# Two adapters of neighbouring half batches in one Gelu task, with a plan of newer durations and newly drawn ranks

## The chip, the cores and the metric

One core of a Trainium2 chip runs the whole kernel in float32. The time is device microseconds of one execution, and of several runs the median counts. The core has five engines with queues of their own: TensorE (PE, matmuls), VectorE (DVE), ScalarE (ACT, which evaluates functions from tables), GpSimd (POOL) and SyncE (SP), which here issues the transfers (DMA). Each engine runs its queue strictly in the order in which the program was written, and waits where a result or a buffer is not there yet.

## What is computed

Eight sequences of 512 tokens with 256 channels pass through four layers. Cut to what matters:

```python
# layer 0, a transformer block with a modulated norm; 16 heads of 16 channels
x = ln(src) * (1 + scale(timestep)) + shift(timestep)
scores = q @ k.T / 4 + attention_bias            # bias: (8, 16, 512, 512)
scores = where(src_mask, -inf, scores)
x = x + softmax(scores) @ v @ Wo + bo
h = ln(x) * g2 + beta2
x = x + gelu2(h @ W1 + b1) @ W2 + b2             # 256 -> 1024 -> 256, gelu2(z) = z*sigmoid(1.702 z)
# layers 1 and 3, the two adapters, each with its own weights
hidden = gelu(x @ down_W.T + down_b)             # 256 -> 64, exact Gelu
hidden = expert_W[idx] @ hidden + expert_b[idx] + domain_emb[idx]   # one of 16 experts a sequence
x = ln(hidden @ up_W.T + up_b + x) * ln_gamma + ln_beta
# layer 2, between the adapters: pairs of channels are rotated by theta and phi of the sequence
```

The first adapter's norm weights and the rotation of layer 2 are folded into one pair of rows for each sequence (`rot`), so a first adapter ends with the rotated tokens and a second one with the output.

## The kernel before

The work is cut by sequence `b`, by half (256 query tokens, two tiles of 128), by group `g` of four heads, and by tile: 8 x 2 x 4 x 2 = 128 units, numbered `n`. `attention` (L908) does one unit: four bias tiles are fetched (L918), the mask is added on POOL (L922), scores are made on PE (L930), subtracted and reduced on DVE (L942), exponentiated on ACT (L946). The result is turned, for two of four heads by PE transposes (L981, all four heads in the first sequence's first three groups) and for the others by DVE and a transfer (L957, L966); every second unit the values are multiplied in (L1007). `prepare` (L778) makes the norm, queries, keys and values of the next sequence.

After every eighth unit, `finish` (L1174) takes the two tiles of a half through the output projection, the feed-forward (L1041, its activations by Tanh at L1070), the first adapter and the second adapter (`adapter`, L1097), and stores them (L1196). The last half is finished one tile at a time (L1299). An adapter with number `l` does, in order:

- at the first half of a sequence, one matmul that joins the chosen expert with the up projection (`eu`, L1103),
- a transpose of the tokens (L744, copied at L702), the down projection (L1116),
- a Gelu for each of the two tiles (L1124), one task of the plan with the mode "gelu",
- the up projection (L768), added to the tokens on DVE (L1133), then statistics (L710 to L719) and norm (L732),
- for `l` = 0 the rotation (L1152, L1156, L1167 or on POOL), for `l` = 1 the norm's weights (L1143).

Nothing is written in the order in which it runs. Every piece is a task with an engine (or a choice of two), a duration, what it reads and writes, and a rank; `Plan.run` (L156) simulates the engines once at build time, gives an engine that comes free the ready task of the lowest rank whose buffers can be had, and the tasks are emitted in that order. Ranks follow the unit: an attention unit's are around `n`; those of a `finish` are spread over n + 2 to n + 11, or n + 19 from n = 100 on, in proportion to its PE work (`Plan.end`, L128, called after L1294). `Plan.stir` (L147) then shifts the ranks in given stretches by random amounts from given seeds; a list of 21 such draws stands at L1303. The plan's constants for transfers are `AFTER[DMA]` (time until a landed transfer is seen), `BACKLOG`, and 1.5 us of landing (L170, L226). The plan counts 1.41 us whenever ACT changes between the modes "exp" and "gelu".

Buffers that matter here come from rings: `HID` has 2 (Gelu outputs), `EU` 2, `HT` 2 (transposed tokens), `RES` 4 (a sequence's tokens), `ROT` 1, and eight PSUM banks, four for scores and four for the rest, which may borrow from the former.

Of the kernel before, what the change touches and what calls it, by code (L numbers as in the profile page):

```python
# [20 lines left out]
P = 128  # L21
# [4 lines left out]
NF = FF // P  # L26
# [4 lines left out]
TURNED = 2  # L31
# [49 lines left out]
class Plan:  # L81

    AFTER = {PE: 0.22, DVE: 0.14, ACT: 0.16, POOL: 0.12, DMA: 2.2}
    BACKLOG = 9.0
    FLIGHT = 8

# [67 lines left out]
    def run(self, free_at):  # L156
        ready = {e: [] for e in free_at}
        mode = dict.fromkeys(free_at)
        events, order, seq = [], [], 0
        for n, t in enumerate(self.tasks):  # L160
            t.n = n
            if t.waits == 0:
                heapq.heappush(events, (t.at, seq, "ready", t))
                seq += 1
        for e, at in free_at.items():
            heapq.heappush(events, (at, seq, "free", e))
            seq += 1
        idle = set()
        now, queues = 0.0, self.BACKLOG
        landed = [self.BACKLOG + 1.5] * self.FLIGHT  # L170
        while events:
            now, _, what, x = heapq.heappop(events)
            if what == "ready":
                for e in x.costs:

                    later = 1.0 if e == DVE and ACT in x.costs else 0.0
                    heapq.heappush(ready[e], (x.rank + later, x.n, x))
            elif what == "free":
                idle.add(x)
            elif what == "over":  # L180
                for b in x.buffers:
                    b.left -= 1
                    if b.left == 0:
                        b.home.free.append(b.slot)
            if events and events[0][0] == now:
                continue
            for e in [e for e in free_at if e in idle]:
                held, short = [], set()
                while ready[e]:
                    entry = heapq.heappop(ready[e])  # L190
                    t = entry[2]
                    if t.engine is not None:
                        continue
                    new = [b for b in t.buffers if b.slot is None]
# [12 lines left out]
                    held.append(entry)  # L207
                else:
                    t = None
                for h in held:  # L210
                    heapq.heappush(ready[e], h)
                if t is None:
                    continue
                for b in new:
                    b.home, b.slot = b.slots.take()
                t.engine, cost = e, t.costs[e]
                if t.mode is not None and t.mode != mode[e]:
                    cost += 1.41 if e == ACT else 0.1
                    mode[e] = t.mode
                idle.discard(e)  # L220
                if e == DMA:
                    begun = now
                    for _ in range(t.many):
                        begun = max(begun, landed[-self.FLIGHT]) + cost / t.many
                        queues = max(queues, begun) + t.data / t.many
                        landed.append(queues + 1.5)  # L226
# [22 lines left out]
def conditioned_sequence_kernel(  # L249
# [320 lines left out]
    def late_weights():  # L570
        wo_rows = w_o.rearrange("(c u j e) n -> c j u e n", c=NC, u=2, e=32)

        def load(rank, cost, data, emit, key, many=1):
# [7 lines left out]
        load(3.0, 3.6, 1.0, lambda: [  # L581
            nc.sync.dma_start(wo[32 * j : 32 * j + 32, c], wo_rows[c, j, :, :HD])
            for c in range(NC) for j in range(4)
        ], "wo", many=8)
# [10 lines left out]
    def rotations():  # L595
# [63 lines left out]
            nc.sync.dma_start(wu[A1:K1, 1], turned_rows)  # L659

        plan.rank = 6.8
        plan(DMA, 1.6, bias_rows, ["turned_rows"], ["wu"], data=0.6, many=4)
        plan.rank = 7.0
        ps = Buffer(BG, lambda t: t[:, : NC * (B + 1)].rearrange("p (c b) -> p c b", c=NC))

# [242 lines left out]
    def attention(u, n):  # L908
# [7 lines left out]
        dif = [Buffer(BIAS) for _ in range(4)]  # L916
        for j in range(4):
            plan(DMA, 0.54, lambda j=j: nc.sync.dma_start(  # L918
                dif[j].t, bias[b, 4 * g + j, qt * P : (qt + 1) * P, :]), [], [dif[j]], data=0.8)
# [49 lines left out]

        if turned:  # L970
            plan(DMA, 2.75, moved, [(tb, j) for j in range(turned)], [(pT, i)],
                 data=1.05 * TURNED, many=4)
        plan.rank = n + 0.0

        whole = "p (j k i q c) -> p j k i q c"
# [119 lines left out]
    eus, rots = {}, {}  # L1095

    def adapter(b, l, res, rk, ts):  # L1097
        n, w = len(ts), len(ts) * P
        rows = slice(ts[0], ts[0] + n)
        if ts[0] == 0:  # L1100

            ps, eu = Buffer(BG, lambda t: t[:A1, :D]), Buffer(EU)
# [1 line left out]
                ps.t, ewT[l][: A1 + 1 + 7 * l, b, :], wu[: A1 + 1 + 7 * l, l, :], start=True,  # L1104
                stop=True), [("ewT", l), "wu", *rk], [ps], mode="full")
            evict(lambda ps=ps: (eu.t, ps.t), [ps], [eu], 0.35, 0.35)
            eus[l] = eu
        eu = eus[l]
        xT, xk = half_transposed(lambda t: res.t[:, t, :], rk, ts)
        ps, hid = Buffer(BG, lambda t: t[:, :P]), Buffer(HID)  # L1110


        def down():
            for c in range(NC):
                for i in range(n):
# [2 lines left out]
                        start=(c == 0), stop=(c == NC - 1),  # L1118
                    )

        def hidden():
            for i in range(n):
                lanes = slice(A * i, A * i + A)
# [2 lines left out]
                    bias=db[lanes, b : b + 1] if l else db[lanes, B:],  # L1126
                )

        plan(PE, 0.52, down, [*xk, "wd"], [ps], mode="down")
        plan(ACT, 0.27 * n, hidden, [ps, "hid1", "db"], [hid], mode="gelu")  # L1130

        def add(ps):
            nc.vector.tensor_tensor(res.t[:, rows], ps, res.t[:, rows], ALU.add)  # L1133
# [7 lines left out]
        if l == 1:  # L1141
            for r, op in enumerate((ALU.mult, ALU.add)):
                plan(DVE, 0.06 + 0.27 * n, lambda r=r, op=op: nc.vector.tensor_tensor(  # L1143
                    hat.t if r == 0 else res.t[:, rows], hat.t, rows_of(rows2, r, n), op),
                    hk if r else ["rows2"], rk if r else hk)
            return


# [25 lines left out]
    def finish(b, ts, store=None):  # L1174
# [13 lines left out]
        if ts[0] == 0:  # L1188
# [14 lines left out]
    def experts_matrices():  # L1203
# [19 lines left out]
        for b in range(B):  # L1223
# [10 lines left out]
                            "o p a -> (o p) a"),  # L1234
                    )

            plan(DMA, 2.0, fetch, ["expert"], [(raw, b)], data=0.2, many=2)

        def kept():
            nc.gpsimd.tensor_tensor(  # L1240
# [43 lines left out]
    for n, u in enumerate(units):  # L1284
# [5 lines left out]
        if n % 8 == 7:  # L1290
            half = n // 8 % 2
            if n + 1 < len(units):
                plan.begin()
                finish(u[0], [2 * half, 2 * half + 1])  # L1294
                plan.end(n + 2.0, n + (11.0 if n < 100 else 19.0))
                continue

            for t in range(2):
                plan.begin()  # L1299
                finish(u[0], [2 + t], Buffer(PT, lambda p: p.rearrange(  # L1300
                    "p (c q) -> p c q", q=2 * P)[:, :NF]) if t else None)
                plan.end(n + 2.0 + 4 * t, n + 11.0 + 4 * t)
    plan.stir([  # L1303
        (410212, 1.8, 6.8, 0.15),
        (199711, 113.2, 123.2, 0.5),
        (682069, 101.9, 121.9, 0.3),
        (105905, 1.0, 6.0, 0.15),
        (778456, 99.8, 104.8, 0.3),
        (979319, 99.1, 139.1, 0.5),
        (907673, 48.8, 68.8, 0.5),  # L1310
        (22724, 102.9, 107.9, 0.5),
        (298360, 122.0, 132.0, 0.3),
        (628414, 41.2, 51.2, 0.5),
        (243383, 126.2, 166.2, 1.0),
        (212106, 116.9, 136.9, 0.3),
        (595484, 120.3, 140.3, 0.15),
        (163641, 56.0, 66.0, 0.3),
        (54223, 41.6, 46.6, 0.15),
        (562752, 129.4, 169.4, 0.5),
        (467595, 24.0, 29.0, 0.3),  # L1320
        (266067, 61.1, 66.1, 0.3),
        (728061, 32.7, 42.7, 0.15),
        (41169, 28.2, 38.2, 0.3),
        (751015, 16.0, 26.0, 0.3),
    ])
    order = plan.run({PE: 1.5, DVE: 2.6, ACT: 3.6, POOL: 1.6, DMA: 5.0})
    for task in order:
# [95 lines left out]
```

## Time and profile before

| | us |
|---|---|
| three runs | 891.4, 893.95, 889.95 (median 891.4) |
| the profiled execution, of which the span | 890.14, 888.4 |
| mean granted TensorE clock | 0.989 of full speed |
| Exp (L946) 512 x 721 ns | 343.6 on ACT |
| copies of transposes (L702) 226 x 584 ns | 125.5 on ACT |
| Gelu (L1124) 64 x 362 ns | 23.2 on ACT |
| mask add (L922) 512 x 1161 ns | 580.3 on POOL |
| ACT waiting for DVE's minimum before an Exp | 45.6, 43 times |
| DVE waiting for scores (L942 for L930) | 31.4, 32 times |
| PE's weight loads waiting for an Exp (L981 for L946) | 20.3, 30 times |
| ACT waiting for a down projection (L1124 for L1116) | 3.4, 5 times |
| transfers, busy share of 16 engines | 78% |

Busy shares are averages over the span. A "wait" is idle time of an engine in front of an instruction, with what ended it; it costs something only where that instruction is on the path to the end, and the chain of work that ended last shows one such path. The 40 slices of the page show a full middle, a dip of the granted clock in the third and fourth slices, and an end in which DVE, ACT and POOL thin out:

```profile
PE   9998999999999999999999999999999999999994
PEld 7654675666666666656666666666666566666683
DVE  4757799989999999988998999899999999999766
ACT  5974779979898998979988897988979789799653
POOL 8867999999899898999889997998899999999432
PEclk9998999999999999999999999999999999999997
DMA  9577887698986988888896978968897898998400
```

### The profile page before, as it was taken

Reading aid. Unit: us, or ns where it says so; the run is one execution under the profiler, and the core shown is the slowest. Engines: PE = TensorE matmul, PEld = TensorE weight load, DVE = VectorE, ACT = ScalarE, POOL = GpSimd, SP = SyncE. Lnnn points to the kernel's source line nnn. Section 1 sums busy time; section 2 is a strip of 40 time slices with the busy share of each in tenths; the row PEclk is TensorE's granted clock in tenths of the full one; section 3 lists DMA queues with packets and bytes.
Section 4 is the critical chain, followed back from the end, with each engine's and each line's share of the span. In section 5 each row is a group of like instructions: output and inputs, shape, how many; then the busy total and the mean of one; then the engine's idle time right before and its main releaser. Section 6 shows DMA issues by size and latency. Waiting matters only on the chain.

```text
span 888.4 us, 20406 instructions
## 1 busy us (share of the span) xinstructions
PE 860.4 (97%) x6430; PEld 565.8 (64%) x6430; DVE 783.0 (88%) x2141; ACT 740.7 (83%) x1349; POOL 775.3 (87%) x907
## 2 busy tenths in 40 slices
PE   9998999999999999999999999999999999999994
PEld 7654675666666666656666666666666566666683
DVE  4757799989999999988998999899999999999766
ACT  5974779979898998979988897988979789799653
POOL 8867999999899898999889997998899999999432
PEclk9998999999999999999999999999999999999997
DMA  9577887698986988888896978968897898998400
GB/s 319 156 226 229 281 254 227 205 293 246 288 276 203 314 276 271 295 243 247 250 317 206 282 238 266 318 202 287 242 309 236 267 284 260 297 298 276 107 25 24
DMA packets 163214, 218.54 MB, mean 246 GB/s; under 512 B 19167, under 2 KB 93961, under 8 KB 163106
## 3 DMA queue, kind: packets, MB, share of 16 engines
q1 hardware_dynamic: 163062, 217.22, 78.0%
q8 instruction: 51, 0.84, 0.4%
q14 instruction: 57, 0.47, 0.2%
q10 hardware_dynamic: 44, 0.02, 0.0%
HBM read 149.89 MB, written 4.24 MB: 173 GB/s over the span
## 4 chain that ended last, share of the span: by engine, by line
PE 56%; ACT 14%; DVE 10%; DMA 8%; POOL 7%; issue 3%; SPq 2%; POOLq 0%; DVEq 0%; ACTq 0%
PE bank L1086 10%; PE bank L930 9%; PE bank L981 8%; PE bank L1061 7%; PE bank L1007 7%; POOL bias L922 5%; DMA bias<-in_bias 5%; ACT bias L946 5%; PE bank L820 4%; DVE bias L942 3%; PE bank L768 3%; ACT pT L702 2%; PE bank L744 2%; PE bank L858 2%; PE bank L419 1%
## 5 line engine op out<-in xcount | busy, mean ns | idle before, releaser
L922 POOL TENSOR_TENSOR bias<-bias,neg 128x512 f32<-128x512 f32 x512 | 580.3, 1161 | 42.3 <-DMA bias<-in_bias 28.2
L946 ACT ACTIVATE bias<-bias,low 128x512 f32<-128x512 f32 x512 | 343.6, 721 | 46.2 <-DVE low L942 45.6
L942 DVE CUSTOM_DVE_ANT_0 bias<-bank,bias 128x512 f32<-128x512 f32 x512 | 328.4, 679 | 42.7 <-PE bank L930 31.4
L981 PEld LDWEIGHTS bank<-shifted,bias 128*128 128x128 f32 x1120 | 124.9, 141 | 77.8 <-ACT bias L946 20.3
L981 PE MATMUL bank<-shifted,bias 128*128 128x128 f32 x1120 | 158.2, 279 | 7.8 <-ACT bias L946 3.2
L957 DVE STREAM_TRANSPOSE tb<-bias 128x512 f32<-128x512 f32 x232 | 155.6, 693 | 4.5 <-ACT bias L946 3.9
L702 ACT COPY pT<-bank 128x512 f32<-128x512 f32 x226 | 125.5, 584 | 35.9 <-PE bank L981 34.1
L930 PE MATMUL bank<-kT,qz 32*128 32x512 f32 x1024 | 149.4, 645 | 0.0
L1007 PE MATMUL bank<-pT,v_pad 128*32 128x256 f32 x1120 | 126.0, 386 | 0.9 <-ACT bias L946 0.9
L1061 PE MATMUL bank<-hT,w 128*128 128x256 f32 (+1 forms) x544 | 125.1, 373 | 1.1 <-ACT hT L754 0.6
L1086 PE MATMUL bank<-w,gT 128*128 128x256 f32 x496 | 119.5, 384 | 0.0
L1007 PE MATMUL bank<-pT,v_turn 128*32 128x256 f32 x928 | 113.1, 386 | 2.0 <-DMA pT<-tb 0.8
L1061 PEld LDWEIGHTS bank<-hT,w 128*128 128x128 f32 x544 | 94.8, 190 | 23.2 <-issue 4.2
L1086 PEld LDWEIGHTS bank<-w,gT 128*128 128x128 f32 x496 | 89.9, 190 | 23.9 <-issue 12.6
L1007 PEld LDWEIGHTS bank<-pT,v_turn 128*32 128x32 f32 x928 | 50.3, 110 | 51.3 <-issue 10.3
L930 PEld LDWEIGHTS bank<-kT,qz 32*128 32x128 f32 x1024 | 42.0, 185 | 42.3 <-issue 27.6
L1070 ACT ACTIVATE sig<-bank,b1s 128x256 f32<-128x256 f32 (+1 forms) x136 | 55.3, 456 | 10.0 <-PE bank L1061 7.2
L1007 PEld LDWEIGHTS bank<-pT,v_pad 128*32 128x32 f32 x1120 | 55.6, 110 | 7.2 <-issue 2.2
L1073 POOL TENSOR_SCALAR sig<-sig 128x512 f32<-128x512 f32 (+1 forms) x68 | 40.1, 593 | 21.8 <-ACT sig L1070 15.8
L1077 DVE SCALAR_TENSOR_TENSOR gT<-bank,cols,sig 128x256 f32<-128x256 f32 (+1 forms) x128 | 54.0, 464 | 4.6 <-POOL sig L1073 4.4
L710 DVE BATCH_NORM_STATS2 st<-res 128x6 f32<-128x256 f32 x128 | 51.4, 410 | 1.7
L718 POOL TENSOR_TENSOR rstd<-rstd,neg_half 128x2 f32<-128x2 f32 (+2 forms) x59 | 43.4, 735 | 4.9
(138 smaller groups left out, 1103.0 us busy)
## 6 DMA issues: line engine op xcount, KB each, us to landing
bias<-in_bias SPq DMA_DIRECT2D x512, 256.0 KB
pT<-tb SPq DMA_DIRECT2D x464, 128.0 KB
out<-res SPq DMA_DIRECT2D x15, 256.0 KB
res<-in_x SPq DMA_DIRECT2D x7, 512.0 KB
v_turn<-v_pad SPq DMA_DIRECT2D x32, 68.0 KB
m<-in_mask SPq DMA_DIRECT2D x8, 256.0 KB
mod<-ada_rows SPq DMA_DIRECT2D x8, 256.0 KB
w<-in_w SPq DMA_DIRECT2D x2, 1024.0 KB
```

Of the source, the lines that this page charges most:

```text
L702: nc.scalar.copy(*pair()) if e == ACT else nc.vector.tensor_copy(*pair())), r, w)
L922: plan(POOL, 1.12, lambda j=j: nc.gpsimd.tensor_tensor(dif[j].t, dif[j].t, negs[qt].t, ALU.add), [negs[qt]], [dif[j]])
L930: nc.tensor.matmul(sc[j].t, qz.t[strip, par, c, qs], kT.t[strip, c, :], start=True, stop=True,)
L942: plan(DVE, 0.61, lambda j=j: nc.vector.tensor_tensor_reduce(dif[j].t, sc[j].t, dif[j].t, -1.0, 3.0e38, ALU.add, ALU.min, low.t[:, j : j + ...
L946: plan(ACT, 0.61, lambda j=j: nc.scalar.activation(dif[j].t, dif[j].t, AF.Exp, bias=low.t[:, j : j + 1], scale=-1.0), [(low, j)], [dif[j]] ...
L957: plan(DVE, 0.62, lambda j=j: nc.vector.transpose(tb.t.rearrange("p (m h k c) -> h p k m c", m=4, h=TURNED, k=NT)[j], dif[j].t.rearrange(" ...
L981: nc.tensor.transpose(ps.t[:, kc, :], dif[j].t[:, kc * P : (kc + 1) * P], ident)
L1007: nc.tensor.matmul(pv.t[32 * j : 32 * j + 32, :], (v_turn if j < turned else v_pad).t[:, at : at + 32], pj, start=(kc == 0), stop=(kc == N ...
L1061: nc.tensor.matmul(ps.t[:, i, :w], w1[:, c, f * P : (f + 1) * P], hT.t[:, c, :w], start=(c == 0), stop=(c == NC - 1),)
L1070: plan(ACT, 0.155 + 0.1 * n, lambda i=i, f=f, ps=ps, sg=sg: nc.scalar.activation(sg.t[:, i, :w], ps.t[:, i, :w], AF.Tanh, bias=b1s[:, f : ...
L1077: plan(DVE, 0.14 + 0.13 * n, lambda i=i, f=f, ps=ps, sg=sg: nc.vector.scalar_tensor_tensor(gT.t[:, f, :w], ps.t[:, i, :w], cols[:, C_B1 + ...
L1086: nc.tensor.matmul(ps.t[:, i, :], gT.t[:, f, i * P : (i + 1) * P], w2[:, f, :], start=(f == 0), stop=(f == NF - 1),)
```

## The change

`adapter` is split in three. `way_down` holds all up to the down projection, `gelus` one ACT task for any number of halves, `way_up` the rest, with the output's store moved into it for `l` = 1. A `finish` now runs the first adapter of its own half together with the second adapter of the half before, which the list `late` remembers; the four Gelus (two tiles each) are one task. The way up of the half's own first adapter is written before that of the older one. Where `last` is set, the half's second adapter follows at once: for n = 119 (n > 110, the last but one) and for the last tile. Joined expert matrices are kept by `(b, l)` instead of `l`.

```diff
-    def adapter(b, l, res, rk, ts):
+    eus, rots, late = {}, {}, []
+
+    def way_down(b, l, res, rk, ts):
...
-            eus[l] = eu
-        eu = eus[l]
+            eus[b, l] = eu
...
+        plan(PE, 0.52, down, [*xk, "wd"], [ps], mode="down")
+
         def hidden():
             for i in range(n):
...
-        plan(PE, 0.52, down, [*xk, "wd"], [ps], mode="down")
-        plan(ACT, 0.27 * n, hidden, [ps, "hid1", "db"], [hid], mode="gelu")
+        return b, l, res, rk, ts, ps, hid, hidden
+
+    def gelus(ways):
+
+        def hidden():
+            for way in ways:
+                way[-1]()
+
+        plan(ACT, 0.27 * sum(len(way[4]) for way in ways), hidden,
+             [*(way[5] for way in ways), "hid1", "db"], [way[6] for way in ways], mode="gelu")
+
+    def way_up(b, l, res, rk, ts, _, hid, hidden):
+        n = len(ts)
+        rows = slice(ts[0], ts[0] + n)
+        eu = eus[b, l]
...
+            plan(DMA, 0.42, lambda: nc.sync.dma_start(
+                out[b].rearrange("(t p) d -> p t d", p=P)[:, rows], res.t[:, rows]), rk, [],
+                data=0.4 * len(ts))
             return
...
-        adapter(b, 0, res, rk, ts)
-        adapter(b, 1, res, rk, ts)
-        plan(DMA, 0.42, lambda: nc.sync.dma_start(
-            out[b].rearrange("(t p) d -> p t d", p=P)[:, rows], res.t[:, rows]), rk, [],
-            data=0.4 * len(ts))
+        ways = [way_down(*way) for way in late]
+        late.clear()
+        ways.append(way_down(b, 0, res, rk, ts))
+        gelus(ways)
+        for way in reversed(ways):
+            way_up(*way)
+        late.append((b, 1, res, rk, ts))
+        if last:
+            way = way_down(*late.pop())
+            gelus([way])
+            way_up(*way)
```

The plan's durations for transfers are changed: `AFTER[DMA]` 2.2 to 2.45; landing 1.5 to 2.0; the output projection's weights (`wo`, L581) 3.6 to 5.3; `bias_rows` (L662) 1.6 to 1.9; an expert's fetch (L1237) 2.0 to 3.1; a bias tile's data (L919) 0.8 to 0.84; that of the turned heads (L972) 1.05 to 0.8 for each. The list of draws has 41 entries in place of 21, three of them over all ranks:

```diff
-        (410212, 1.8, 6.8, 0.15),
-        (199711, 113.2, 123.2, 0.5),
...
+        (905035, -99.0, 9999.0, 0.15),
+        (96033, -99.0, 9999.0, 0.15),
+        (609436, -99.0, 9999.0, 0.15),
+        (919282, 99.8, 119.8, 1.0),
...
```

More of the change, by code (lines that the diff above doesn't have):

```diff
@@ L81 @@
 class Plan:
-    AFTER = {PE: 0.22, DVE: 0.14, ACT: 0.16, POOL: 0.12, DMA: 2.2}
+    AFTER = {PE: 0.22, DVE: 0.14, ACT: 0.16, POOL: 0.12, DMA: 2.45}
     BACKLOG = 9.0
@@ L169, in run @@
         now, queues = 0.0, self.BACKLOG
-        landed = [self.BACKLOG + 1.5] * self.FLIGHT
+        landed = [self.BACKLOG + 2.0] * self.FLIGHT
         while events:
@@ L225, in run @@
                         queues = max(queues, begun) + t.data / t.many
-                        landed.append(queues + 1.5)
+                        landed.append(queues + 2.0)
                     cost = begun - now
@@ L580, in late_weights @@
             bv_row, rows_in[R_BV * D : (R_BV + 1) * D].partition_broadcast(P)), "bv")
-        load(3.0, 3.6, 1.0, lambda: [
+        load(3.0, 5.3, 1.0, lambda: [
             nc.sync.dma_start(wo[32 * j : 32 * j + 32, c], wo_rows[c, j, :, :HD])
@@ L661, in rotations @@
         plan.rank = 6.8
-        plan(DMA, 1.6, bias_rows, ["turned_rows"], ["wu"], data=0.6, many=4)
+        plan(DMA, 1.9, bias_rows, ["turned_rows"], ["wu"], data=0.6, many=4)
         plan.rank = 7.0
@@ L918, in attention @@
             plan(DMA, 0.54, lambda j=j: nc.sync.dma_start(
-                dif[j].t, bias[b, 4 * g + j, qt * P : (qt + 1) * P, :]), [], [dif[j]], data=0.8)
+                dif[j].t, bias[b, 4 * g + j, qt * P : (qt + 1) * P, :]), [], [dif[j]], data=0.84)
         plan.rank = n - 1.6
@@ L971, in attention @@
             plan(DMA, 2.75, moved, [(tb, j) for j in range(turned)], [(pT, i)],
-                 data=1.05 * TURNED, many=4)
+                 data=0.8 * TURNED, many=4)
         plan.rank = n + 0.0
@@ L1093, in feed_forward @@
             res.t[:, here], ps.t[:, :n], res.t[:, here], ALU.add), [ps], rk)
-    eus, rots = {}, {}
-    def adapter(b, l, res, rk, ts):
-        n, w = len(ts), len(ts) * P
-        rows = slice(ts[0], ts[0] + n)
+    eus, rots, late = {}, {}, []
+    def way_down(b, l, res, rk, ts):
+        n = len(ts)
         if ts[0] == 0:
@@ L1127, in hidden @@
                 )
-        plan(PE, 0.52, down, [*xk, "wd"], [ps], mode="down")
-        plan(ACT, 0.27 * n, hidden, [ps, "hid1", "db"], [hid], mode="gelu")
+        return b, l, res, rk, ts, ps, hid, hidden
[6 more added lines that the diff above has]
+    def way_up(b, l, res, rk, ts, _, hid, hidden):
+        n = len(ts)
+        rows = slice(ts[0], ts[0] + n)
+        eu = eus[b, l]
         def add(ps):
@@ L1172, in adapter, with finish @@
              [(tmp, 0), (tmp, 1)], rk)
-    def finish(b, ts, store=None):
+    def finish(b, ts, store=None, last=False):
         res, keys = state[b][0], state[b][1]
@@ L1235, in fetch @@
                     )
-            plan(DMA, 2.0, fetch, ["expert"], [(raw, b)], data=0.2, many=2)
+            plan(DMA, 3.1, fetch, ["expert"], [(raw, b)], data=0.2, many=2)
         def kept():
@@ L1293, in conditioned_sequence_kernel @@
                 plan.begin()
-                finish(u[0], [2 * half, 2 * half + 1])
+                finish(u[0], [2 * half, 2 * half + 1], last=n > 110)
                 plan.end(n + 2.0, n + (11.0 if n < 100 else 19.0))
@@ L1300, in conditioned_sequence_kernel @@
                 finish(u[0], [2 + t], Buffer(PT, lambda p: p.rearrange(
-                    "p (c q) -> p c q", q=2 * P)[:, :NF]) if t else None)
+                    "p (c q) -> p c q", q=2 * P)[:, :NF]) if t else None, t == 1)
                 plan.end(n + 2.0 + 4 * t, n + 11.0 + 4 * t)
     plan.stir([
-        (410212, 1.8, 6.8, 0.15),
-        (199711, 113.2, 123.2, 0.5),
[L1306 to L1323, printed above, removed]
@@ L1324, in conditioned_sequence_kernel @@
-        (751015, 16.0, 26.0, 0.3),
+        (905035, -99.0, 9999.0, 0.15),
+        (96033, -99.0, 9999.0, 0.15),
+        (609436, -99.0, 9999.0, 0.15),
+        (919282, 99.8, 119.8, 1.0),
+        (904339, 59.9, 69.9, 0.3),
+        (446272, 114.2, 119.2, 0.3),
+        (820841, 59.1, 69.1, 0.15),
+        (216068, -1.6, 3.4, 0.5),
+        (220218, 107.9, 112.9, 0.5),
+        (578800, 10.7, 20.7, 0.5),
+        (856081, 6.6, 16.6, 0.15),
+        (322583, 0.1, 5.1, 1.0),
+        (559531, 18.3, 58.3, 1.0),
@@ new lines, in conditioned_sequence_kernel @@
+        (562631, 119.9, 124.9, 0.15),
+        (769648, 22.8, 27.8, 0.15),
+        (581098, 52.3, 92.3, 1.0),
+        (8149, 52.0, 57.0, 0.3),
+        (279057, -2.9, 2.1, 0.5),
+        (885486, 81.9, 86.9, 0.5),
+        (573854, 1.1, 11.1, 0.15),
+        (328849, 36.4, 41.4, 0.15),
+        (45663, 82.4, 87.4, 0.5),
+        (348383, 107.2, 117.2, 0.3),
+        (901769, 97.4, 102.4, 0.15),
+        (260395, 88.2, 93.2, 0.3),
+        (257885, 94.3, 99.3, 0.15),
+        (38702, 112.0, 117.0, 0.15),
@@ new lines, in conditioned_sequence_kernel @@
+        (908404, 90.8, 95.8, 0.15),
+        (717976, -0.8, 9.2, 0.15),
+        (444136, 68.4, 73.4, 0.15),
+        (657233, 0.0, 5.0, 1.0),
+        (50612, -2.6, 7.4, 0.15),
+        (673631, 65.1, 70.1, 0.15),
+        (606584, 25.3, 30.3, 0.3),
+        (265603, 129.9, 149.9, 0.5),
+        (316770, 0.2, 5.2, 1.0),
+        (551299, 66.7, 71.7, 0.15),
+        (790891, 50.6, 55.6, 0.3),
+        (552312, 60.9, 65.9, 0.15),
+        (527436, 18.5, 23.5, 0.3),
+        (31783, 0.3, 5.3, 1.0),
```

## The prediction

> **What bounds the kernel now.** I read the busy shares first, then the windows, then the chain of work that ended last, and last the timelines of ScalarE and of the end.
>
> ```profile
> PE 860.4 (97%) x6430; PEld 565.8 (64%) x6430; DVE 783.0 (88%) x2141; ACT 740.7 (83%) x1349; POOL 775.3 (87%) x907
> ...
> PE 56%; ACT 14%; DVE 10%; DMA 8%; POOL 7%; issue 3%; SPq 2%; POOLq 0%; DVEq 0%; ACTq 0%
> ```
>
> No engine bounds it alone. PE looks full, but its ends are modelled and only 56% of the chain lies on it: the rest is work that PE's queue, whose order is fixed, stood waiting for. ScalarE (ACT) has the least to do of the four, yet after PE the largest share of the chain.
>
> ```profile
> 50.00:100.00 50.00, 44.10 (x328) 25.29 (x327) 33.41 (x89) 27.85 (x49) 35.16 (x39) 0.90 0.75 244
> ...
> 500.00:550.00 50.00, 49.93 (x390) 33.64 (x388) 47.32 (x129) 43.53 (x79) 43.51 (x52) 1.00 0.86 265
> ...
> 845.00:888.40 43.40, 31.84 (x198) 25.38 (x197) 28.31 (x82) 19.38 (x55) 14.64 (x37) 0.89 0.08 25
> ```
>
> The columns after the stretch and its length are PE, PEld, DVE, ACT and POOL busy, then clock, DMA share and GB/s. Three regimes: a start that is poorly filled (50 to 100 us), a long middle, and an end. Summed over the eleven stretches from 250 to 800 us, DVE is busy 514.5 of 550 us (94%), POOL 509.7 (93%), ACT 488.5 (89%). So in the middle ACT is the third of three engines that are nearly full.
>
> **Part 1, fewer table loads.** ScalarE changes its function table whenever a Gelu follows an Exp, and again on the way back:
>
> ```profile
> L946 ACT ACT_TABLE_LOAD x27 | 34.6, 1283 | 0.5
> L1124 ACT ACT_TABLE_LOAD x27 | 34.6, 1283 | 0.4
> ```
> ```profile
> 296.65 1.33 ACT L946 ACTIVATE bias<-bias,low 128x512 f32<-128x512 f32 x2
> 297.99 1.28 ACT L1124 ACT_TABLE_LOAD   x1
> 299.29 0.74 ACT L1124 ACTIVATE hid<-bank,db 64x128 f32<-64x128 f32 x2
> 300.05 0.58 ACT L702 COPY pT<-bank 128x512 f32<-128x512 f32 x1
> 300.65 1.28 ACT L946 ACT_TABLE_LOAD   x1
> ```
>
> Counting Gelu groups in ScalarE's timeline: the 13 half batches of n = 7 to 103 have two each (26), that of n = 111 has its first at 835 us, and everything later follows the last Exp (833 us) and needs no load. That makes 27 loads into Gelu; the 27 into Exp are 26 ways back and the one at the start. After the change the finishes of n = 7 to 111 have one task each: 14 loads into Gelu, and 13 back plus the start, 14 into Exp (15 if an Exp still follows the last of them). So 54 - 28 = 26 loads go, 26 x 1.283 = 33.4 us of ScalarE, which falls to about 707 us. The 64 Gelus (0.36 us) stay. That the four really share one table is seen in the kernel before at 850.10 us, where four Gelus of two half batches stood together by chance: 1.51 us with no load between.
>
> How much of 33.4 us is on the path? In the chain I added the pieces that are table loads: seven of those into Gelu and five back, 8.8 + 6.4 = 15.2 us of 69.3, or 22%. The whole engine gives a lower rate: 121.9 us of chain for 740.7 us busy, 16%. Times 33.4 us these are 7.3 and 5.5. The bounds are 0 (all of it falls into ACT's idle time, 888.4 - 740.7 = 147.7 us, covered by DVE and POOL) and 33.4 (all on the path, which the 22% speaks against). I take **-6.4 us**, the middle of the two rates, since they are measured on this very resource.
>
> The Trainium skill (ScalarE: Activation LUTs, "What ACT_TABLE_LOAD costs") gives the load the same 1283 ns, but adds a drain of about 1380 ns to each. The rows above show no such drain: 297.98 to 297.99, then 299.27 to 299.29. By the page 26 switches would be 69 us of ScalarE and, at 22%, 15 us of the time.
>
> Against the change speaks Perfetto Trace Analysis, "Identifying the Most-Contended Engine", in the same skill: the engine with the highest occupancy is the one to work on. By it ACT at 83% behind DVE at 88% is the wrong one, and this part would be worth about nothing.
>
> **Part 2, the longer task and its wait.** A Gelu task now holds ScalarE for 2 x 1.28 + 4 x 0.37 = 4.0 us instead of 3.3, half as often: the Exps of the next unit queue behind it, and the transposes on PE behind them. Its wait is for both down projections. In the middle the older one costs nothing: its input is ready about one half batch earlier (from 298 to 347 us in the Gelu loads, some 50 us), and that head start is the cover. Without cover the task would wait as long as the later one does, which it does in any case. Before, Gelus found ScalarE idle for only 3.4 us in five places. Waits of PE for a Gelu's result (8.0 us, 15 times) should roughly halve, but are in the chain's rate already. Bounds -4 to +4; I take **0**. The out stores go with the second adapter, one issue each as before, about 50 us later on SP's queue; that queue's waits for DVE in front of them are large at the end only. Four RES tiles hold a batch for about three batches' time, which suffices; every other instruction count is unchanged: 0.
>
> **Part 3, the end.** Here the cover is gone. The second adapter of tile 2 of the last half now shares a task with the first of tile 3.
>
> ```profile
> 871.32 0.36 ACT L1124 ACTIVATE hid<-bank,db 64x128 f32<-64x128 f32 x1 [0.27 <-PE bank L1116]
> 871.83 0.75 ACT L1124 ACTIVATE hid<-bank,db 64x128 f32<-64x128 f32 x2 [0.15 <-PE bank L1116]
> ...
> 874.39 0.36 ACT L1124 ACTIVATE hid<-bank,db 64x128 f32<-64x128 f32 x1 [0.59 <-PE bank L1116]
> ...
> 880.10 0.36 ACT L1124 ACTIVATE hid<-bank,db 64x128 f32<-64x128 f32 x1 [1.27 <-PE bank L1116]
> ```
>
> Tile 3's first Gelu is that of 871.32, tile 2's second that of 874.39; with one task and the same order the former would wait 3.1 us and stand behind one more Gelu: +3.4. Since the last chain runs from tile 3's first adapter to its second (880.10) and the end, late there is late at the end. The least is one Gelu, +0.4, if tile 2 is put earlier. I take **+2.0**, because DVE works on the other half until 875.6 us and hides part.
>
> **Part 4, durations and ranks.** No instruction is added; the order on all queues changes. The newer numbers are closer to the trace in at least one place I can check:
>
> ```profile
> 37.85 5.49 SPq L582 DMA_DIRECT2D wo<-in_w_o  x8
> ```
>
> The plan had 3.6 us here and now has 5.3. SP's queue and late transfers are what the chain shows from 50 to 100 us (37.2% DMA bias, 17.5% SP issues of pT and bias). There DVE does 33.4 us against 46.8 per 50 us in the middle, so 13.4 us is the most that a better order could win there; a worse one could cost the same elsewhere, since every fixed queue is redrawn. Bounds -13.4 to +13.4; I take **-3.0**, a fifth of the best, as only some of the durations bear on this place.
>
> **Sum.** -6.4 + 0 + 2.0 - 3.0 = -7.4 us. The profiled execution took 890.14 us, its span 888.4 and 1.7 around it; after: span 881.0, execution 882.7. The median of the three runs is 891.4, 1.3 above, so the time to compare is **884.0 us**.
>
> **Rivals.** A measurement of this kernel can tell about 0.5%, 4.5 us, from no change.
>
> *Faster, as summed* (870 to 886.9): chance **0.53**.
>
> *No change: the loads come out of idle time.* DVE and POOL at 94 and 93% pace the middle, and what ACT gains it waits away for "DVE low" (already 45.6 us before its Exps). Part 1 is then 0, and 2.0 - 3.0 leaves 890.4 us. For it: the occupancies. Against: twelve table loads lie on the chain itself. Chance **0.16** (886.9 to 895.9).
>
> *Slower: the joint task blocks ScalarE's queue.* If the current half's down product comes late by t, the load and the wait stand at the head of ScalarE's queue with the next unit's Exps behind; DVE, PE and the bias buffers starve in turn. It happens 14 times. It decides from 14 t > 7.4 + 4.5, t = 0.85 us. The longest such idle before was at 193 us, 1.1; at 1.3 us each it is +18.2, and 884.0 + 18.2 = 902.2 us. For it: at 469 to 477 us of the trace before, the queue stays in the Gelu table for 7.6 us without an Exp, and an order drawn anew can put this at any half. Against: only five of 34 tasks waited at all, and the older half's product is never the late one in the middle. Chance, with everything else in a redrawn order that ends slower, **0.31**.
>
> That the change doesn't do what it says I leave out: the four Gelus are one task, so nothing can stand between them.
>
> **Numbers.** The likeliest is 884.0; its own range is 870 to 886.9. The range for 8 in 10 goes from 868 (parts 1 and 4 at 7.3 and 13.4, part 3 at 0.4, gives 891.4 - 20.3 = 871.1, and some more if the start and the middle both gain) to 902 (the slower rival); about 0.1 is left out at each end. Both signs hold much of the chance. Faster by over 0.5% 0.53, within 0.16, slower 0.31.
>
> **What would show it.** Table loads 28 or 29 in place of 54, ACT busy near 707 us, 14 Gelu groups of about 1.5 us up to the last Exp: part 1 was done. Its worth: the loads' share of the chain falls from 15.2 us to about 8, and the time between two Gelu groups (some 52 us a half batch) shrinks by some 0.4 us. Part 2 is wrong if "ACT hid" waiting for the down bank rises well above 3.4 us, or if "PE transposes waiting for ACT bias" (20.3 us) grows. Part 3: from PE's last second-layer matmul (869.1 us) to the end, 19.3 us before, about 2 us more after. Part 4: DVE's 33.4 us in the window of 50 to 100 us rises. The prediction is wrong if the middle runs no faster, or if the start or the end loses more than the middle wins.

## The result, and the profile after

| | median us | lowest to highest | runs |
|---|---|---|---|
| before | 889.7 | 887.2 to 894.0 | 10 |
| after | 897.6 | 890.3 to 899.4 | 10 |

The ratio is 1.0078, with a 95% interval of 1.0053 to 1.0103: the change made the kernel slower, by about 7 us. 884.0 was predicted; the measured time lies inside the range of 868 to 902, on the other side of no change.

The page's busy row and chain of the kernel after:

```profile
PE 861.2 (96%) x6430; PEld 567.7 (63%) x6430; DVE 777.8 (87%) x2138; ACT 710.4 (79%) x1326; POOL 775.1 (86%) x907
...
PE 55%; ACT 13%; POOL 11%; DMA 9%; DVE 7%; issue 4%; SPq 1%; POOLq 0%; ACTq 0%; DVEq 0%
```

ScalarE lost 30.3 us of work, and the span grew by 9.1 (888.4 to 897.5). ScalarE's groups and one of its joint tasks:

```profile
L946 ACT ACT_TABLE_LOAD x14 | 18.0, 1283 | 0.2
L1123 ACT ACT_TABLE_LOAD x14 | 18.0, 1283 | 0.2
```
```profile
303.05 1.28 ACT L1123 ACT_TABLE_LOAD   x1
304.35 1.50 ACT L1123 ACTIVATE hid<-bank,db 64x128 f32<-64x128 f32 x4
305.87 0.20 ACT L724 ACTIVATE minus<-mv 128x2 f32<-128x2 f32 x1
306.10 1.28 ACT L946 ACT_TABLE_LOAD   x1
```

28 loads in place of 54, four Gelus in 1.50 us: the change does what it says. ScalarE's idle time grew by 39.4 us (30.3 + 9.1). Where it lies is in the list of waits (engine and line that waited, what it waited for: us in total, times, longest):

```profile
ACT bias L946 <- DVE low L942: 73.9, 63, 8.4
...
PEld bank L981 <- ACT bias L946: 31.1, 42, 5.5
...
ACT hid L1123 <- PE bank L1113: 3.5, 3, 1.9
```

Before, the first row was 45.6 us. Its rise, 28.3 us, is close to the 30.3 us that ScalarE lost in work, but that doesn't show that the one turned into the other, since the order of the queues changed too; experiment 1 takes them apart. The second row, PE's transposes waiting for an Exp, was 20.3 us before. The third, the joint task's wait for its down projections, is 3.5 us in place of 3.4.

The windows, to set beside those of before (stretch and length, then PE, PEld, DVE, ACT, POOL busy, clock, DMA share, GB/s):

```profile
50.00:100.00 50.00, 41.66 (x310) 23.30 (x309) 30.79 (x85) 25.01 (x42) 36.22 (x39) 0.90 0.76 236
...
500.00:550.00 50.00, 50.00 (x392) 33.92 (x391) 46.03 (x128) 42.52 (x81) 47.50 (x55) 1.00 0.85 260
...
850.00:897.50 47.50, 33.64 (x207) 27.24 (x205) 28.96 (x83) 20.76 (x59) 15.75 (x40) 0.87 0.09 29
```

The start is no better (DVE 30.8 us between 50 and 100, 33.4 before). As a measure for progress I took from the traces the end of every fourth Exp, that is of each unit:

| | unit 16 | unit 64 | unit 96 | last Exp (unit 128) | last second-layer matmul | end of span |
|---|---|---|---|---|---|---|
| before | 128.3 | 436.6 | 644.1 | 833.8 | 869.1 | 888.4 |
| after | 129.2 | 441.6 | 647.1 | 837.1 | 875.4 | 897.5 |

In this pair 3.3 us are lost up to the last Exp and 5.8 behind it: 54.6 us became 60.4.

The end after the change, ScalarE's Gelus (compare the four rows of before at 871.32 to 880.10):

```profile
877.78 0.75 ACT L1123 ACTIVATE hid<-bank,db 64x128 f32<-64x128 f32 x2 [0.42 <-PE bank L1113]
880.41 0.62 ACT L1123 ACTIVATE hid<-bank,db 64x128 f32<-64x128 f32 x2 [1.88 <-PE bank L1113]
...
889.26 0.36 ACT L1123 ACTIVATE hid<-bank,db 64x128 f32<-64x128 f32 x1 [1.25 <-PE bank L1113]
```

The joint Gelu of tiles 2 and 3 stands at 880.41, 5.0 us behind the last second-layer matmul; tile 3's stood 2.2 us behind it before (871.32 for 869.1). Counted from the last Exp on, 14 Gelus are left after the change and 12 before.

One statement ahead of the prediction has to be put right: `last` is set not only for n = 119 but for n = 111 too, since 111 > 110. That half finishes with three adapters: the older half's second, its own first, its own second. The number of Gelus behind the last Exp doesn't depend on it: the two that came in addition are those of the older half's second adapter.

### The profile page after: what moved, and what is told of

Its sections match the earlier page's. It is cut to its first block, busy times and chain, and to the rows that moved or that the text cites. A ratio compares the mean times of both kernels' runs of the same rounds, so it can differ in the third digit from the quotient of the medians.

```text
span 897.5 us, 20329 instructions
## 1 busy us (share of the span) xinstructions
PE 861.2 (96%) x6430; PEld 567.7 (63%) x6430; DVE 777.8 (87%) x2138; ACT 710.4 (79%) x1326; POOL 775.1 (86%) x907
## 3 DMA queue, kind: packets, MB, share of 16 engines
q1 hardware_dynamic: 163062, 217.22, 77.3%
## 4 chain that ended last, share of the span: by engine, by line
PE 55%; ACT 13%; POOL 11%; DMA 9%; DVE 7%; issue 4%; SPq 1%; POOLq 0%; ACTq 0%; DVEq 0%
PE bank L930 10%; PE bank L981 9%; PE bank L1061 8%; PE bank L1007 7%; POOL bias L922 7%; PE bank L1086 7%; DMA bias<-in_bias 7%; PE bank L820 5%; ACT bias L946 4%; PE bank L768 3%; DVE bias L942 3%; ACT pT L702 2%; POOL rstd L718 1%; PE bank L744 1%; PE bank L858 1%
## 5 line engine op out<-in xcount | busy, mean ns | idle before, releaser
L946 ACT ACTIVATE bias<-bias,low 128x512 f32<-128x512 f32 x512 | 346.3, 720 | 74.4 <-DVE low L942 73.9
L981 PEld LDWEIGHTS bank<-shifted,bias 128*128 128x128 f32 x1120 | 127.0, 142 | 79.7 <-ACT bias L946 31.1
L981 PE MATMUL bank<-shifted,bias 128*128 128x128 f32 x1120 | 160.0, 278 | 11.6 <-ACT bias L946 8.2
L930 PE MATMUL bank<-kT,qz 32*128 32x512 f32 x1024 | 152.2, 643 | 0.5 <-DVE low L942 0.5
L702 ACT COPY pT<-bank 128x512 f32<-128x512 f32 x219 | 123.2, 582 | 34.9 <-PE bank L981 33.0
L1086 PE MATMUL bank<-w,gT 128*128 128x256 f32 x496 | 119.0, 383 | 0.4 <-ACT pT L702 0.4
L1086 PEld LDWEIGHTS bank<-w,gT 128*128 128x128 f32 x496 | 90.1, 190 | 23.9 <-issue 13.4
```

Of the source, the lines that this page charges most:

```text
L702: nc.scalar.copy(*pair()) if e == ACT else nc.vector.tensor_copy(*pair())), r, w)
L930: nc.tensor.matmul(sc[j].t, qz.t[strip, par, c, qs], kT.t[strip, c, :], start=True, stop=True,)
L946: plan(ACT, 0.61, lambda j=j: nc.scalar.activation(dif[j].t, dif[j].t, AF.Exp, bias=low.t[:, j : j + 1], scale=-1.0), [(low, j)], [dif[j]] ...
L981: nc.tensor.transpose(ps.t[:, kc, :], dif[j].t[:, kc * P : (kc + 1) * P], ident)
L1086: nc.tensor.matmul(ps.t[:, i, :], gT.t[:, f, i * P : (i + 1) * P], w2[:, f, :], start=(f == 0), stop=(f == NF - 1),)
```

## The experiments

Each ratio is to the kernel before on the same chip, with its 95% interval; the median of before was 889.4 to 890.4 us in all of these.

**1. The loads alone, in the same order.** Tanh needs no load after an Exp (one of the 54 loads is left in the run), and the plan's task keeps its cost and mode, so that no queue changes:

```diff
-                    hid.t[:A, i * P : (i + 1) * P], ps.t[lanes], AF.Gelu,
+                    hid.t[:A, i * P : (i + 1) * P], ps.t[lanes], AF.Tanh,
```

> The kernel before, with Tanh in place of the adapters' Gelu (the output changes with it). Tanh shares the Exp's table, so 52 of 54 table loads go (about 67 us of ScalarE) while every queue keeps its order. Theory A, the loads lie in ScalarE's idle time: 0 to -3 us. Theory B, the loads are on the path at the 22% that the chain shows and the change lost its gain to a worse order: about -15 us.

> The changed kernel, likewise with Tanh in place of the adapters' Gelu (the output changes with it): 26 of its 28 table loads go, in the same order of all queues. Theory A: 0 to -2 us against the changed kernel (ratio to the kernel before 1.006 to 1.008). Theory B: about -8 us (8.5 us of its chain are loads), ratio 0.999.

Before with Tanh: 0.9977 (0.9960 to 0.9994), -2.0 us, with 53 loads gone (one more than was expected). After with Tanh: 1.0050 (1.0026 to 1.0074), 2.5 us under the changed kernel's ratio, with overlapping intervals; this lies a little beyond theory A's range and far from theory B's 0.999. The page of before with Tanh, and three of its waits:

```profile
PE 858.7 (97%) x6430; PEld 565.8 (64%) x6430; DVE 782.3 (88%) x2141; ACT 675.8 (76%) x1296; POOL 775.7 (88%) x907
```
```profile
ACT bias L946 <- DVE low L942: 53.9, 55, 3.8
ACT pT L702 <- PE bank L981: 44.9, 41, 3.9
ACT minus L724 <- DVE mv L712: 39.1, 30, 5.1
```

ScalarE has 64.9 us less to do (740.7 to 675.8) and the kernel gains 2.0: 3%, not 22%. The time is waited away in front of the next instruction that needs another engine (45.6 to 53.9, 34.1 to 44.9 and 21.4 to 39.1 us in these three rows). Theory A holds: in a given order nearly all of the loads were hidden.

The runs with Tanh also answer for the two rows that grew in the changed kernel. VectorE's "low" rose by 8.3 us when 53 loads went in the same order. In the changed kernel it is 77.3 us without loads, 73.9 with them. So with no loads on either side the row still differs by 23.4 us (53.9 and 77.3): most of its rise came with the new order, not with the freed time. The transposes' wait is 30.9 us there without loads, 31.1 with them, so it isn't the loads in front of the Exps that make it either.

**2. The coupling of the last two tiles.**

```diff
-                    "p (c q) -> p c q", q=2 * P)[:, :NF]) if t else None, t == 1)
+                    "p (c q) -> p c q", q=2 * P)[:, :NF]) if t else None, True)
```

> The changed kernel, but the second adapter of the last half's first tile follows its own first adapter instead of sharing a task with the next tile's. Theory, the coupling at the end costs what the stretch from PE's last second-layer matmul to the end grew by (19.3 to 22.1 us): -2.8 us, ratio about 1.005. Rival, the stretch grew because more work was left over at the last Exp and not by the coupling: 0, ratio 1.008.

Measured 1.0051 (1.0032 to 1.0071), which looks like the first theory, but the profile denies it: from the last second-layer matmul to the end it took 21.9 us, as against 22.1 coupled and 19.3 before, and from the last Exp to the end 60.1. Tile 3's first Gelu did come earlier:

```profile
874.31 0.36 ACT L1123 ACTIVATE hid<-bank,db 64x128 f32<-64x128 f32 x1 [0.79 <-PE bank L1113]
876.65 0.36 ACT L1123 ACTIVATE hid<-bank,db 64x128 f32<-64x128 f32 x1 [0.74 <-PE bank L1113]
877.19 0.72 ACT L1123 ACTIVATE hid<-bank,db 64x128 f32<-64x128 f32 x2
885.28 0.36 ACT L1123 ACTIVATE hid<-bank,db 64x128 f32<-64x128 f32 x1 [1.76 <-PE bank L1113]
```

It stands 2.6 us behind the matmul (874.31, the matmul ended at 871.7), but its second is 11.0 us later (8.8 before). So the coupling isn't what makes the end longer. That run is 2 us faster than the changed kernel because its last Exp came earlier (833.4 for 837.1).

**3. The deferral at the end.** The second adapter follows at once from n = 95 on (and for both last tiles):

```diff
-                finish(u[0], [2 * half, 2 * half + 1], last=n > 110)
+                finish(u[0], [2 * half, 2 * half + 1], last=n > 94)
```

> The changed kernel, but from n = 95 on every half runs its second adapter at once again, as in the kernel before (the joint task is kept up to there). Theory, the end is longer because one adapter more is left over at the last Exp: from the last Exp to the end about 54 us, like the kernel before (54.6), in place of 60.4. Rival, the end is longer for another reason: 60. The ranks from n = 95 on fall on other tasks, so the time of the whole (up to 10 us either way) is not what is asked here.

From the last Exp to the end 55.4 us, as the theory has it: with the one adapter more gone, the end is short again. As a whole it was slower, 1.0147 (1.0101 to 1.0194): the last Exp came only at 848.0 us, probably because the draws found for the end now shift other tasks.

**4. Structure, durations and draws apart.** Old or new adapters, old or new durations, all with the list taken out (`plan.stir` left off), and the new adapters with the old durations and the old list:

> The kernel before without its list of draws (same adapters, same durations). It shows what the 21 draws are worth. If a redrawn order matters by more than the table loads: slower than before by 5 us or more. If not: within 3 us.

> The new adapters (joint Gelu task) with the old durations and no draws. Against the same with the old adapters: theory A, the structure is worth nothing or a little: 0 +- 4 us. Theory B, it is worth what was predicted and the redrawn order ate it: -4 us or more.

> The old adapters with the new durations and no draws. Against the old durations without draws: if the newer durations fit the chip better, faster by 3 us or more (part 4 as predicted); if they make no better order, within 3 us or slower.

> The changed kernel without its list of draws. If the 41 new draws are worth something on the chip, this is slower than the changed kernel (ratio above 1.012); if they only fit the plan's own model, it is about the same (1.004 to 1.012) or faster.

> The new adapters with the durations and the list of draws of the kernel before. If the new structure itself costs (some 6 us at the end and up to 5 in the middle) and draws are worth something only for the tasks for which they were found: 908 to 915 us. If the structure is neutral and only the draws matter: about 898, as the old adapters without draws.

| adapters | durations | list | ratio (interval) | median us |
|---|---|---|---|---|
| old | old | none | 1.0084 (1.0054 to 1.0115) | 898.3 |
| new | old | none | 1.0272 (1.0235 to 1.0308) | 914.1 |
| old | new | none | 1.0324 (1.0287 to 1.0361) | 918.6 |
| new | new | none | 1.0344 (1.0310 to 1.0378) | 922.3 |
| new | old | old | 1.0306 (1.0254 to 1.0358) | 918.0 |

What a list is worth exceeds anything the loads could give: 21 draws 8.4 us in the old kernel (898.3 to 889.9), 41 draws 24.7 us in the new one (922.3 to 897.6). And it is worth this only for the tasks for which it was found: the old list makes the new adapters no faster than none (918.0 and 914.1). Without draws the new adapters lost 15.7 us under the old durations and 3.7 under the new, and the new durations lost 20.3 us with the old adapters, 8.2 with the new. An order can thus differ by as much as 20 us with the same instructions. Two of these runs fell outside all that was expected of them: for the new adapters without draws neither theory had a loss of 15.7 us, and with the old list 918.0 is above the highest forecast, 915.

The same runs bear on the end. Without draws it takes 56.5 and 56.7 us with the old adapters (old and new durations), 65.3 and 64.5 with the new ones: the deferral makes it longer there by about 8 us.

**5. Which durations.** The base is the first row of the table.

```diff
-        load(3.0, 3.6, 1.0, lambda: [
+        load(3.0, 5.3, 1.0, lambda: [
...
-    AFTER = {PE: 0.22, DVE: 0.14, ACT: 0.16, POOL: 0.12, DMA: 2.2}
+    AFTER = {PE: 0.22, DVE: 0.14, ACT: 0.16, POOL: 0.12, DMA: 2.45}
```

The first run has the former and the two other start durations, the second the latter and the landing of 2.0.

> The old adapters without draws and the old durations, but the three start durations new (output weights 5.3, bias rows 1.9, expert fetch 3.1). If numbers nearer to the trace make a better start, as part 4 of the prediction had it: the tenth unit is done earlier than at 88.5 us, and the time is under 898 us. If they are what made the newer durations lose 20 us: tenth unit at 92 us or later, 908 us or more.

> The same base, but only the latency of transfers new (2.45 and 2.0 in place of 2.2 and 1.5). If this is what cost: 908 us or more. If the start durations are: within 5 us of 898.

Start durations (output weights, bias rows, expert fetch): 1.0240 (1.0193 to 1.0287), 912.5 us, tenth unit at 93.5 (88.5 without them) and the 64th at 450.6 (443.8). Latency: 1.0154 (1.0108 to 1.0200), 903.3 us, tenth unit at 85.6. The start durations, of which the prediction had held that of the output weights against the trace, made the start worse, not better. The latency isn't free either: it cost 5 us.

**6. Equal effort.** For old and new adapters, and for the new ones with the deferral ended early (`last=n > 102`, both last tiles), all with the old durations, lists were found from nothing by about the same number of trials (3,300 to 3,500), judged by the end time that the plan itself computes:

> The old adapters and the old durations, with a list of draws found anew (21 kept of 3,300 tried by the end time that the plan itself computes, which is 858.4 us). The plans run so far ended on the chip 30 to 33 us above their own end for the old adapters: 889 to 892 us, the same as the kernel before. If its list had been better for a reason outside the plan: 895 us or more.

> The new adapters and the old durations, with a list found by the same effort (36 draws of 3,400, the plan's end 858.6). Theory A, the structure is worth nothing once both are drawn equally, since its gain in the middle is given back at the end: 889 to 896 us, last Exp some 3 us earlier and the end 4 to 6 us longer than in the old adapters' run. Theory B, it is worth the predicted 6 us and the change lost it by its list and durations: 883 to 886. Rival C, the chip runs the new structure worse than the plan thinks (the two runs with the old durations were 37 us above the plan): 895 us or more.

> The joint task up to n = 95, and from n = 103 on (the half after it) every half runs its second adapter at once; old durations, list found by the same effort (26 draws of 3,500, the plan's end 858.2). If the longer end was the whole loss: from the last Exp to the end 54 to 56 us and 886 to 890 us in all. Rival C: 895 us or more.

| | ratio (interval) | median us | last Exp | from there to the end |
|---|---|---|---|---|
| old adapters | 1.0062 (1.0028 to 1.0096) | 895.7 | 835.9 | 59.0 |
| new adapters | 1.0043 (1.0018 to 1.0069) | 893.4 | 834.6 | 59.5 |
| new, ended early | 1.0059 (1.0032 to 1.0086) | 894.1 | 836.9 | 55.7 |

The busy rows of the first and the second:

```profile
PE 862.1 (96%) x6430; PEld 565.5 (63%) x6430; DVE 780.5 (87%) x2134; ACT 745.3 (83%) x1356; POOL 777.0 (87%) x907
```
```profile
PE 860.7 (96%) x6430; PEld 568.2 (64%) x6430; DVE 780.0 (87%) x2139; ACT 711.9 (80%) x1325; POOL 777.1 (87%) x907
```

ScalarE has 33.4 us less in the second, as much as 26 loads take, and the three times can't be told apart. Equally drawn, the joint task is worth nothing that this measurement sees, as theory A had it for the time. Its details missed: the old adapters' end was as long here (59.0) with no adapter left over, so an order alone can stretch the end by 4.5 us (54.6 before), and the short end of the third run made it no faster. PE's transposes, whose wait for an Exp had grown in the changed kernel, wait less here with the joint task (16.0 us) than without (27.8).

This comparison has a limit: it is one list for each. The kernel before is some 5 us faster than its own adapters drawn anew, although their plans end within 1.6 us of each other, so lists that the plan holds equal can differ on the chip by nearly what was predicted for the loads. A gain of a few us could hide in that; that the loads themselves are worth little rests on experiment 1. Why the list of the kernel before suits the chip better isn't shown. No kernel with the full computation beat it.

The plan's own end beside the chip, for the kernels with their own plan (us):

```text
before 856.8 -> 889.7      old, old, none 866.8 -> 898.3      old_start   882.4 -> 912.5
after  867.5 -> 897.6      new, old, none 877.4 -> 914.1      old_latency 871.5 -> 903.3
split  867.4 -> 895.5      old, new, none 887.7 -> 918.6      old_drawn   858.4 -> 895.7
early  872.3 -> 904.2      new, new, none 890.7 -> 922.3      new_drawn   858.6 -> 893.4
                           new, old, old  880.6 -> 918.0      early_drawn 858.2 -> 894.1
```

The chip is 28 to 37 us above the plan in all fourteen, and the plan itself saw the changed kernel end 10.7 us later than the one before.

**7. What paces the middle.** Time is taken off one resource at a time, in the order of the kernel before. The first two halve the columns of one operation:

```diff
-                dif[j].t, dif[j].t, negs[qt].t, ALU.add), [negs[qt]], [dif[j]])
+                dif[j].t[:, :D], dif[j].t[:, :D], negs[qt].t[:, :D], ALU.add), [negs[qt]], [dif[j]])
```
```diff
-                dif[j].t, sc[j].t, dif[j].t, -1.0, 3.0e38, ALU.add, ALU.min,
+                dif[j].t[:, :D], sc[j].t[:, :D], dif[j].t[:, :D], -1.0, 3.0e38, ALU.add, ALU.min,
```

> The kernel before, in the same order, but the mask is added to half of each bias tile only (256 of 512 columns; the rest of the mask is left out), which takes some 250 us off GpSimd. If GpSimd paces the middle, so that ScalarE's freed time could show nowhere: faster by 20 us or more. If the order of waits between all engines paces it and not one engine: faster by less than 10 us, little more than the 2 us that 65 us of ScalarE gave.

> The kernel before, in the same order, but the scores are subtracted and reduced over half of each tile only (256 of 512 columns; the Exp's scale is set so that the untouched half stays finite), which takes some 140 us off VectorE. If VectorE paces the middle: faster by 20 us or more. If not: less than 10 us.

The next two halve the terms of the second layer and the bias transfers:

```diff
-                    for f in (f0, f0 + 1):
+                    for f in (f0,):
```
```diff
-                dif[j].t, bias[b, 4 * g + j, qt * P : (qt + 1) * P, :]), [], [dif[j]], data=0.8)
+                dif[j].t[:, :D], bias[b, 4 * g + j, qt * P : (qt + 1) * P, :D]), [], [dif[j]], data=0.8)
```

> The kernel before, in the same order, but the second matmul of the feed-forward takes every other one of its eight terms (half of its products are left out), which takes some 60 us off PE (half of 119.5 + 3.8). If PE itself paces the middle, its 97% being real and not only modelled: faster by 35 us or more. If the fixed order of waits paces it, as with the other three engines (65 us of ScalarE gave 2, some 120 of VectorE 4, some 240 of GpSimd 5): less than 10 us.

> The kernel before, in the same order, but each bias tile's transfer brings 256 of its 512 columns (the other half of the bias is left out; the 15 buffers are cleared once at the start, some 3 us of GpSimd), which takes 67 of 150 MB of reads away. If the transfers pace the middle: faster by 20 us or more. If no single engine or queue does, and it is the chain of waits through all of them in a fixed order: less than 10 us, as for the other four.

| less of | by | ratio (interval) | us |
|---|---|---|---|
| ScalarE (experiment 1) | 64.9 us | 0.9977 (0.9960 to 0.9994) | -2.0 |
| GpSimd | 243 us | 0.9940 (0.9913 to 0.9967) | -5.3 |
| VectorE | 118.5 us | 0.9951 (0.9928 to 0.9974) | -4.4 |
| PE | about 55 us | 0.9977 (0.9949 to 1.0005) | -2 |
| transfers | 67 MB of reads | 0.9934 (0.9913 to 0.9956) | -5.9 |

The busy rows of the runs with less GpSimd, and with less VectorE:

```profile
PE 856.4 (97%) x6430; PEld 564.0 (64%) x6430; DVE 782.8 (88%) x2141; ACT 739.2 (84%) x1349; POOL 532.2 (60%) x907
```
```profile
PE 857.2 (97%) x6430; PEld 564.1 (64%) x6430; DVE 664.5 (75%) x2141; ACT 740.6 (83%) x1349; POOL 774.9 (87%) x907
```

and of the run with less PE, with the two groups of its matmuls that moved; behind them the same groups before (248 of L1086's matmuls are gone, and 8 of a smaller group of that line for the last tile, 1.4 us):

```profile
PE 847.2 (95%) x6174; PEld 535.1 (60%) x6174; DVE 782.0 (88%) x2141; ACT 743.2 (83%) x1349; POOL 775.2 (87%) x907
```
```profile
L930 PE MATMUL bank<-kT,qz 32*128 32x512 f32 x1024 | 178.3, 640 | 0.9 <-DVE low L942 0.7
...
L1086 PE MATMUL bank<-w,gT 128*128 128x256 f32 x248 | 66.0, 389 | 0.2 <-DVE gT L1077 0.2
```
```profile
L930 PE MATMUL bank<-kT,qz 32*128 32x512 f32 x1024 | 149.4, 645 | 0.0
L1086 PE MATMUL bank<-w,gT 128*128 128x256 f32 x496 | 119.5, 384 | 0.0
```

No relief of a single resource, by the amounts in the table, brings more than 6 us; all five are in the order of the kernel before. That the waits through the other engines hold the time is the reading that is left; no run relieved two at once. Even PE, which the page calls 97% busy, could lose 53.5 us in one group while its busy time fell by 13.2 only (that profile has a granted clock of 0.983, 0.989 before): the scores' group grew by 28.9 us with the same 1024 matmuls. A single one of them took no longer (640 ns, 645 before), so fewer of them ran at the same time. PE's busy time is therefore no measure of its work alone.

## Why the prediction was wrong, point by point

- *What bounds it.* "No engine bounds it alone" was right, and more thoroughly so than it was used: five resources were relieved one by one for about 2 to 6 us (experiment 7). The prediction should have drawn its price from this sentence.
- *Part 1, the loads.* Count (28), ScalarE's busy time (710.4 for 707) and the group's shape held. The step of the prediction that failed is "-6.4 us, the middle of the two rates, since they are measured on this very resource". A piece's share of one chain that ended last says that it lay on that path, not that the end moves when it goes: another path can end a little earlier, and in experiment 1 the loads that held 15.2 us of the chain were worth 2.0 (0.5 to 3.6) when 53 of 54 went. The prediction's sign for this part didn't come either: the loads' share of the chain was to fall to about 8 us and the middle to run faster, but nine loads hold 11.1 us of the chain after, and from unit 16 to the last Exp it took 707.9 us, 705.5 before. The rival "no change: the loads come out of idle time" had the mechanism, though not the time (897.6 lies above its 895.9). That the row it named, VectorE's "low", grew by 28.3 us is mostly luck: 23.4 us of the difference stand without any loads too.
- *The two pages of the Trainium skill.* Perfetto Trace Analysis ("Identifying the Most-Contended Engine") says to work first on the engine with the highest occupancy; from this the prediction read that ScalarE's relief is worth about nothing, and experiments 1 and 6 agree (-2.0 us of 64.9; equal at 33.4). But the rule doesn't help here: the relief of VectorE and GpSimd, which are busier, gave 4.4 and 5.3 us. ScalarE: Activation LUTs ("What ACT_TABLE_LOAD costs") adds a drain of about 1.38 us to a load; the rows after show none either (304.33 to 304.35 us).
- *Part 2, the task and its wait.* Its price of 0 fits: 3.5 us of waiting in place of 3.4. The other sign it gave for being wrong did appear, PE's transposes waiting for an Exp (31.1 us for 20.3), but not by the joint task: the wait stays without loads (30.9), and at equal effort it is shorter with the joint task (16.0 for 27.8). The slower rival, a blocked ScalarE queue, did not happen; the time went its way by what it added in half a sentence, a redrawn order that ends slower.
- *Part 3, the end.* "+2.0" from the coupling: from the last matmul to the end it did grow by 2.8 us, but experiment 2 denies the cause. What failed is that the work left over was not counted: one adapter of two tiles more is pending at the last Exp. The whole end grew by 5.8 us; with the deferral ended early it is 55.4 (experiment 3), and without draws the deferral adds about 8 (experiment 4). An order alone can do nearly as much, as the 59.0 of the old adapters drawn anew shows.
- *Part 4, durations and ranks.* "-3.0, a fifth of the best" had the wrong sign. The reason given, a duration nearer to the trace, was tested together with the two other start durations, without draws, and cost 14.2 us (898.3 to 912.5). "Every fixed queue is redrawn" was noted, and its size, 8 to 25 us for a list, not measured or feared enough: it is larger than any term of the sum.
- *What the loss consists of.* In the profiled pair 5.8 us lie in the end, for which the leftover adapter is the likeliest cause, and 3.3 before the last Exp, where the 2 us that the loads are worth were lost with some more to the new order. By medians, the new adapters with the old durations and a list drawn for them take 893.4 us; from there to the changed kernel's 897.6 it is the new durations and their list, and between it and the 889.7 of before lies no more than the old adapters lose too when they are drawn anew (895.7). That the joint task itself is neutral is seen at equal effort only for the old durations, with one list each. Open stays why the list of the kernel before runs 5 us better than others of the same plan end, and which tasks of it do so.

## What to carry to other kernels

Where several engines are nearly full and every queue's order is fixed, the price of a saving is not its share of the chain: take the saved work out in the same order (another function from the same table, half the columns) and see what the end does. A change that makes a planner draw its order anew is mostly that, a new order; compare it with the old code drawn anew by the same effort, not with the best list known, and with several lists each, since two that the plan held equal lay 5 us apart here. When work is deferred, count what is left over when the main stream ends.

## What was not expected of the hardware

PE's busy time in a profile hardly falls when matmuls are taken away: 256 of 6430 gone, about 55 us by their own groups' rows, and 13.2 us less busy, while another group's 1024 matmuls spread over 28.9 us more without any single one taking longer. Halving the bytes of the largest transfer brought reads from 149.9 to 82.8 MB and gave 5.9 us.
